# Flamingo gated block on one core: row centring and one rounding cast on GpSimd, and the last quarter of a hand-laid order laid anew

## The chip, the cores and the metric

The kernel runs on one core of one Trainium2 chip. The metric is device time of one execution in microseconds (us), the median of several runs. The engines are called as in the profile: PE (TensorE matmul) with PEld (its weight loads), DVE (VectorE), ACT (ScalarE), POOL (GpSimd) and SP (SyncE, which here only issues DMAs).

## What is computed

The reference, cut to what matters (16 sequences of 224 rows, 512 wide; a context of 750 rows of 384 each, masked at its end; 8 heads of 64; a feed-forward of 2048):

```python
def attention(x, context, mask, W_q, W_k, W_v, W_o, b_o):
    q, k, v = heads(x @ W_q), heads(context @ W_k), heads(context @ W_v)
    sim = where(mask, q @ k.T * 64**-0.5, -max)
    return merge(softmax(sim) @ v) @ W_o + b_o

def bitlinear(x, w, b):                     # ternary weights, rows in 8 bits
    xq = act_quant(rmsnorm(x))              # scale 127 / max|row|, round
    return xq @ weight_quant(w).T + b

x = x + tanh(g_xattn) * attention(layernorm(x), ctx, mask, ...)
n = layernorm(x)
x = x + tanh(g_ffn) * bitlinear(gelu(bitlinear(n, w1, b1)), w2, b2)
```

## The kernel before

The 3584 rows of `x` are 28 tiles of 128 rows, in 14 pairs (0 to 13). Keys that the mask removes are not gathered, so a sequence (a "slot" s, 0 to 15, sorted by length) has at most `CAPS[s]` keys. Attention goes by slot: context transposes (`ctxp`), keys (`kp`), values (`vp`, `vr`), queries (`qp`), scores (`sim`), row maxima with the mask on DVE (`max`), exponentials on ACT (`exp`), reciprocals on DVE (`rec`), the division on POOL (`mul`, L1426), transposes of the probabilities (`ptp`, evicted by `pT`), the weighted sum (`av`, evicted by `xoT`, two halves one after the other).

The rest goes by pair i and tile k (named `step.i.k`):

- `op`: output projection on PE (L1547); `ya`: its gate and residual into `y` on DVE (L1554); `bs`: row mean and variance on DVE (L1591, L1592).
- `fx` (L1595 to L1600): rows less their mean, 128x512, which ACT or DVE writes.
- `ax` (row maximum of |fx|, L1605, and its scale), `xi` (scaled rows to int16, L1614) on DVE; `xq`: these integers cast to bf16 by ACT (L1014) or DVE (L1012); `xqT`: transposed, by a DMA from SP's queue (L1627), and for pair 13 by PE (`xqp`, L1655) and an ACT copy (L1659).
- `c1`: five small POOL instructions for the row scales; `yb`: bias added into `y` on POOL (L1646).
- `hp.i.k.g`: up projection, half g of the 2048 columns, 8 matmuls of 512 columns on PE (L1671); `h`: its eviction with scale and bias on DVE (L1682); `gelu` on ACT (L1726; for pair 13 in halves, L1778); `ah` or `am`: row maximum on DVE (L1731, L1783); `hi`: scaled rows to int16, 128x2048, on DVE (L1737).
- `hq` (L1739 to L1742): those integers cast to bf16, 128x2048, by ACT or DVE as the order says; `hqT`: transposed by a DMA from SP's queue (L1748); for tile 12.0 and pair 13 by halves on PE (`hqp`, L1709) and an ACT copy (L1713). `sq`: row squares on ACT; `c2`: row scales on POOL.
- `fp`: down projection, 16 matmuls (L1908; for 12.0 and pair 13 in two halves `fp.i.k.g`); `yf`: scale and residual on DVE (L1931); `out`: rows to memory, by an indirect DMA from POOL up to pair 11 (L1940) and from SP's queue after (L1938).

Every step is a small function kept by name. The string `ORDER` lists 2263 names; the program is the steps called in that order, and a suffix `:s` or `:v` sends an eviction or cast to ACT or DVE:

```python
names = ORDER.split()
with tc.manual_schedule():
    for name in names:
        key, _, on = name.partition(":")
        steps[key](*on)
```

So each engine's queue is the list with the other engines' steps left out, and an engine never passes over an instruction that waits. What steps of different engines wait for is data and buffers. Two rings of PSUM matter: `ps_sim` has two wide buffers, which `sim`, `av` and `hp` take in turn, so each waits for the eviction of the one before the last; `ps_gen` has four for all else.

Of the kernel before, what the change touches and what calls it, by code (L numbers as in the profile page):

```python
# [12 lines left out]
ALU = mybir.AluOpType  # L13
# [40 lines left out]
wd.1.0 load.b2 pT.1.1.r:s keys.4 ptr.1.2 pT.1.2:s wq.1.7 ptp.1.3 wT.1.2:s ptr.1.3 op.0.0 wi.1.5 wd.1.7 wT.1.6:s wq.1.5
max.2.0.0 wd.1.5 load.b1 gates wT.1.3:s pT.1.3.r:v max.2.0.1 pT.1.2.r:v pT.1.3:s stats.4.1 wT.1.0:s av.1 max.2.0.2
wT.1.1:s wT.1.7:v wT.1.5:s max.2.0.3 ctxp.3.0 ind.5 xoT.1.1:s y.0.0 sim.2.2 xoT.1.0:s ctxp.3.2 exp.2.0.2 sim.2.3 y.0.1
exp.2.0.3 op.0.1 exp.2.0.1 max.2.2.0 exp.2.0.0 max.2.2.3 max.2.3.0 ctxT.3.0:s yo.0.0 max.2.2.2 exp.2.2.3 max.2.2.1
exp.2.2.2 ctxT.3.2:v max.2.3.2 yo.0.1 ya.0.0 exp.2.3.2 sim.2.1 exp.2.2.0 rec.2.0 pi.5 stats.5.0 mul.2.0 kp.3.0
# [3 lines left out]
mul.2.1 ptr.2.2 vr.3 pT.2.2.r:s rec.2.3 mask.3 qT.3.0:s mul.2.3 fx.0.1:s sim.3.0 kT.3.2:s ax.0.0 sim.3.1 v_rest.3:s  # L62
ptr.2.1 ptp.2.1 pT.2.1.r:s ptp.2.2 xi.0.0 c1.0.0 pT.2.1:s ptp.2.3 max.3.0.0 pT.2.2:s ctxp.4.0 xi.0.1 ptr.2.3 exp.3.0.0
qp.3.2 max.3.1.0 xq.0.0:s max.3.0.2 yb.0.1 max.3.1.3 pT.2.3.r:s xqT.0.0 max.3.0.1 pT.2.3:s max.3.0.3 ctx.5.0 exp.3.0.1
max.3.1.1 exp.3.0.2 max.3.1.2 pi.6 av.2 stats.5.1 rstd.4 ctxT.4.0:s exp.3.1.3 ind.7 exp.3.0.3 norm.4.0 y.1.1 xnp.7
xoT.2.0:s hp.0.0.0 xnT.7.4:s xoT.2.1:s exp.3.1.1 hp.0.0.1 qT.3.2:s h.0.0.0 rec.3.0 keys.6 mul.3.0 hp.0.1.0 h.0.0.1
yo.1.1 gelu.0.0 ptp.3.0 h.0.1.0 xnp.8 ptr.3.0 ctxp.4.2 norm.4.1 sim.3.2 pT.3.0:v sim.3.3 x.6.0 max.3.2.0 op.1.0
max.3.3.0 max.3.3.2 xnT.8.5:s y.2.0 exp.3.1.0 max.3.3.3 max.3.2.1 max.3.2.3 yo.1.0 max.3.2.2 exp.3.1.2 max.3.3.1
ah.0.0 xnT.8.4:s hp.0.1.1 exp.3.2.3 exp.3.3.3 exp.3.2.2 qp.4.0 pT.3.0.r:s exp.3.2.0 h.0.1.1 exp.3.2.1 exp.3.3.0 hi.0.0
ctxT.4.2:s exp.3.3.2 exp.3.3.1 op.1.1 rec.3.1 stats.6.0 gelu.0.1 mul.3.1 rec.3.2 ya.1.0 x.6.1 rec.3.3 mul.3.3 kp.4.0  # L70
qT.4.0:s ya.1.1 mul.3.2 ptr.3.1 kT.4.0:v kT.4.0.c:s ptp.3.1 ptp.3.3 pT.3.1.r:s bs.1.1 ptr.3.3 yb.0.0 pT.3.3:s vp.4
# [4 lines left out]
exp.4.0.3 xqT.1.0 exp.4.1.3 exp.4.0.1 xnp.10 yf.0.0 x.7.1 fp.0.1 xnT.10.6:s ind.8 exp.4.0.0 rstd.6 exp.4.1.2  # L76
xnT.10.5:s exp.4.1.0 c1.1.0 exp.4.1.1 rec.4.0 stats.7.0 hp.1.0.0 qT.4.2:v mul.4.0 yf.0.1 hp.1.0.1 h.1.0.0 ctx.6.0
ptp.4.0 h.1.0.1 yo.2.1 hp.1.1.0 pT.4.0:s gelu.1.0 out.0.1 hp.1.1.1 h.1.1.0 yo.2.0 ctxp.5.0 h.1.1.1 sim.4.3 yb.1.0
# [5 lines left out]
ptr.4.3 v_rest.5:v ptp.4.1 fx.2.1:v fp.1.0 mask.5 max.5.0.0 ax.2.0 sq.1.1 hqT.1.1 xi.2.0 qp.5.2 xi.2.1 pT.4.1:s c2.1.1  # L84
max.5.0.3 pT.4.3.r:s max.5.1.0 xq.2.0:s max.5.0.2 yf.1.0 xqT.2.0 max.5.0.1 kp.5.2 rec.4.2 exp.5.0.1 max.5.1.3 mul.4.2
exp.5.0.3 max.5.1.1 max.5.1.2 xnp.11 yb.1.1 kT.5.2.c:s fp.1.1 qT.5.2:s kT.5.2:s ctx.6.1 xnT.11.6:s x.8.0 c1.2.0 xnp.12
yf.1.1 ptr.4.2 xnT.12.7:s hp.2.0.0 exp.5.1.1 xnT.12.6:s exp.5.0.2 yb.2.1 hp.2.0.1 pT.4.2.r:s h.2.0.0 exp.5.0.0
exp.5.1.0 out.1.1 exp.5.1.2 ptp.4.2 h.2.0.1 exp.5.1.3 pi.8 xnp.13 pT.4.2:s ctxp.6.0 sim.5.3 rec.5.0 ctxT.6.0:s mul.5.0
av.4 gelu.2.0 max.5.3.0 max.5.3.3 keys.8 max.5.3.1 yo.3.0 rec.5.1 max.5.3.2 hp.2.1.0 x.9.0 xoT.4.0:v xoT.4.1:v yo.3.1
# [5 lines left out]
max.6.1.0 mul.5.2 stats.9.0 pT.5.3.r:s kT.6.2:s pT.5.3:s max.6.0.1 yb.2.0 hq.2.1:v ptr.5.2 ptp.5.2 ax.3.0 pT.5.2.r:s  # L95
hqT.2.1 vr.6 yo.4.0 exp.6.0.1 pT.5.2:s exp.6.0.2 av.5 ind.9 x.9.1 qT.6.2:s c2.2.0 xi.3.0 fp.2.0 max.6.1.1 c1.3.0
xi.3.1 xq.3.0:v stats.8.0 xqT.3.0 max.6.1.2 c2.2.1 exp.6.1.2 pi.9 fp.2.1 exp.6.0.0 keys.9 max.6.1.3 xoT.5.0:s
v_rest.6:v exp.6.0.3 y.4.1 ind.10 exp.6.1.1 xoT.5.1:s x.8.1 hp.3.0.0 yf.2.0 ctx.8.0 norm.7.0 hp.3.0.1 h.3.0.0 rec.6.0
mul.6.0 xnp.14 h.3.0.1 hp.3.1.0 xnT.14.8:s yf.2.1 gelu.3.0 ptp.6.0 out.2.1 h.3.1.0 ctxp.7.0 sim.6.2 yb.3.0 op.4.0
max.6.2.0 max.6.2.3 max.6.2.1 exp.6.2.0 yo.4.1 ctxT.7.0:v max.6.2.2 ah.3.0 yb.3.1 pT.6.0:s exp.6.2.1 ctxp.7.2 sim.6.3  # L100
norm.7.1 exp.6.2.3 ptr.6.0 exp.6.2.2 op.4.1 out.2.0 exp.6.1.0 hi.3.0 exp.6.1.3 ya.4.0 sq.3.0 rec.6.2 max.6.3.0 mul.6.2
bs.4.0 qp.7.0 ya.4.1 y.5.0 hq.3.0:v fx.4.0:v hqT.3.0 max.6.3.2 max.6.3.3 hp.3.1.1 qT.7.0:s rec.6.1 mul.6.1 pT.6.0.r:s
# [7 lines left out]
v_rest.7:s ptp.7.0 ah.4.0 rstd.8 hq.3.1:s ptr.7.0 op.5.1 norm.8.1 max.7.2.0 hqT.3.1 max.7.3.0 max.7.2.2 c2.3.1  # L110
# [3 lines left out]
hq.4.0:v hqT.4.0 mul.7.3 ptr.7.1 x.10.1 yf.3.1 kp.8.0 pT.7.1.r:v fx.5.1:v ptr.7.2 kT.8.0:s ptp.7.1 ax.5.0 ptr.7.3  # L114
pT.7.2.r:s sim.8.0 pT.7.1:s sim.8.1 pT.7.3.r:s ptp.7.2 sq.4.0 mask.8 c1.5.0 max.8.0.0 ptp.7.3 max.8.0.2 qp.8.2
stats.10.0 pT.7.3:s xi.5.0 norm.8.0 max.8.1.0 pT.7.2:s max.8.0.3 max.8.1.3 yb.4.1 exp.8.0.3 max.8.1.1 kp.8.2
stats.10.1 yb.5.1 max.8.1.2 xnp.17 xi.5.1 fp.4.0 xnT.17.9:s yb.4.0 xnT.17.10:s max.8.0.1 xq.5.0:v exp.8.0.1 ah.4.1
xqT.5.0 exp.8.0.2 out.3.1 qT.8.2:s av.7 hi.4.1 y.6.0 xnp.16 xoT.7.0:s hp.5.0.0 y.6.1 xnT.16.9:v xoT.7.1:s sq.4.1
c2.4.0 hp.5.0.1 h.5.0.0 exp.8.1.0 exp.8.0.0 hp.5.1.0 h.5.0.1 kT.8.2:v gelu.5.0 hp.5.1.1 h.5.1.0 rec.8.0 yf.4.0 mul.8.0
vp.8 hq.4.1:v rstd.9 exp.8.1.1 ah.5.0 hqT.4.1 ptp.8.0 norm.9.1 qp.9.0 v.8:s yo.6.1 h.5.1.1 c2.4.1 pT.8.0:v gelu.5.1  # L120
sim.8.2 sim.8.3 max.8.2.0 yo.6.0 op.6.0 qT.9.0:v max.8.2.2 max.8.2.3 out.4.0 hi.5.0 exp.8.2.3 yb.5.0 max.8.2.1
# [802 lines left out]
def compact_path(ctx, tc, sh, x, context, out, late_rows, stages):  # L924
# [3 lines left out]
    nc = tc.nc  # L928
# [14 lines left out]
    NPAIR = NTOK // 2  # L943
# [628 lines left out]
    def normalise(i, ks=(0, 1)):  # L1572
        f = pairs[i]
# [144 lines left out]
    def gelu(i, k):  # L1718
# [20 lines left out]
        @step("hq", i, k)  # L1739
        def run(on):  # L1740
            hq = f["hq", k]
            cast(on, hq, hq.bitcast(I16))  # L1742
# [473 lines left out]
```

## Time and profile before

| what | value |
|---|---|
| median of 3 runs | 658.07 us (657.64 to 658.19) |
| the profiled execution's own time | 658.56 us |
| its span (first to last instruction) | 656.8 us |
| PE, PEld busy | 633.6 us (96%), 411.8 us (63%) |
| DVE, ACT, POOL busy | 494.2 us (75%), 434.7 us (66%), 380.8 us (58%) |

Busy time of an engine is a share of the whole span. The last 55 us have another make-up than the rest: attention is over, and PE has two pairs of the feed-forward left, whose rows must pass DVE, ACT and POOL before PE can go on.

### The profile page before, as it was taken

What the parts mean: (1) busy time and instruction counts of PE and PEld (TensorE: products, weight loads), DVE (VectorE), ACT (ScalarE), POOL (GpSimd) and SP (SyncE); (2) the same over time, 40 slices, a digit from 0 to 9 for tenths busy, and PEclk for the clock granted to TensorE, in tenths of its full rate; (3) what the DMA queues carried; (4) which work ended last, traced back from release to release, by engine and by line L of the source; (5) the groups of instructions that cost most, each with busy time, mean ns of one, the idle gap of its engine ahead of it and who ended that gap; (6) DMA issues with size and microseconds to landing.
All of it is one profiled execution on the core that took longest, in us unless ns stands there. A gap on an engine that the chain in (4) does not pass through costs nothing.

```text
span 656.8 us, 11053 instructions
## 1 busy us (share of the span) xinstructions
PE 633.6 (96%) x3706; PEld 411.8 (63%) x3706; DVE 494.2 (75%) x1325; ACT 434.7 (66%) x985; POOL 380.8 (58%) x531
## 2 busy tenths in 40 slices
PE   6989899999999999999999999999999999999995
PEld 5767757767566585675756668656666755654442
DVE  6798788776874787777878577886595865858994
ACT  2489786767676673596757467875496554859694
POOL 6444558664866447663757763753776364564741
PEclk9999999999999999999999999999999999999999
DMA  6959682116233053312235521513243041433222
GB/s 204 371 81 304 196 199 69 45 49 110 66 87 86 32 80 91 84 34 61 65 77 80 96 75 34 92 46 58 64 117 73 17 97 50 95 65 81 48 33 86
DMA packets 97346, 60.73 MB, mean 92 GB/s; under 512 B 85461, under 2 KB 85609, under 8 KB 97152
## 3 DMA queue, kind: packets, MB, share of 16 engines
q1 hardware_dynamic: 89232, 35.41, 25.8%
q0 software_dynamic: 8048, 24.53, 12.4%
q8 instruction: 31, 0.51, 0.3%
q14 instruction: 35, 0.29, 0.1%
HBM read 31.87 MB, written 7.34 MB: 60 GB/s over the span
## 4 chain that ended last, share of the span: by engine, by line
PE 84%; DVE 6%; DMA 5%; ACT 2%; issue 1%; POOL 1%; DVEq 0%; POOLq 0%
PE hp L1671 14%; PE fp L1908 14%; PE qp L1345 14%; PE op L1547 13%; PE kp L1180 5%; PE vp L1207 5%; PE sim L1378 5%; PE ptp L1448 3%; PE av L1488 3%; DMA raw<-w 2%; PE xnp L1323 2%; DMA raw<-in_L_ffn_w_dram 2%; PE vr L1224 1%; DMA x<-in_x_dram,token 1%; PE ctxp L1160 1%
## 5 line engine op out<-in xcount | busy, mean ns | idle before, releaser
L1426 POOL TENSOR_TENSOR p<-p,rec 112x752 f32<-112x752 f32 (+13 forms) x64 | 73.2, 1149 | 134.4 <-DVE rec L1421 101.6
L1409 ACT ACTIVATE p<-p,nm 112x188 f32<-112x188 f32 (+13 forms) x256 | 102.0, 401 | 26.8 <-DVE nm L1395 25.8
L1345 PE MATMUL qp<-xnT,wq_sb 128*128 128x224 f32 x512 | 103.2, 355 | 0.0
L1671 PE MATMUL hp<-w1T,xqT 128*128 128x512 fp8e4 x448 | 102.1, 379 | 1.1 <-DVE h L1682 0.7
L1908 PE MATMUL fp<-w2T,hqT 128*128 128x512 fp8e4 x448 | 100.9, 379 | 0.7 <-ACT hqT L1713 0.7
L1547 PE MATMUL op<-wo_sb,xoT 128*128 128x512 f32 x224 | 101.0, 596 | 0.0
L1345 PEld LDWEIGHTS qp<-xnT,wq_sb 128*128 128x128 f32 x512 | 95.4, 190 | 4.9 <-issue 2.9
L1682 DVE SCALAR_TENSOR_TENSOR h<-hp,c,b_bc 128x1024 f32<-128x1024 f32 x52 | 66.6, 1282 | 31.3 <-PE hp L1671 26.5
L1671 PEld LDWEIGHTS <-xqT 128*128 128x128 bf16 x448 | 43.5, 98 | 51.3 <-issue 3.4
L1908 PEld LDWEIGHTS <-hqT 128*128 128x128 bf16 x448 | 43.1, 98 | 49.9 <-issue 1.1
L1547 PEld LDWEIGHTS op<-wo_sb,xoT 128*128 128x128 f32 x224 | 41.0, 190 | 44.7 <-issue 43.5
L1395 DVE CUSTOM_DVE_ANT_0 p<-sim,mask 112x64 f32<-112x64 f32 (+12 forms) x224 | 54.9, 281 | 18.7 <-PE sim L1378 12.0
L1731 DVE TENSOR_REDUCE a<-h 128x1 f32<-128x2048 f32 x26 | 59.2, 2277 | 1.1 <-ACT h L1726 1.1
L1726 ACT ACTIVATE h<-h 128x2048 f32<-128x2048 f32 x26 | 49.7, 1913 | 11.6 <-DVE h L1682 11.4
L1180 PE MATMUL kp<-ctxT,wk_sb 128*128 128x188 f32 (+12 forms) x360 | 52.4, 295 | 0.9 <-ACT pT L1025 0.9
L1180 PEld LDWEIGHTS kp<-ctxT,wk_sb 128*128 128x128 f32 x360 | 49.2, 191 | 5.9 <-issue 3.3
L1025 ACT COPY pT<-ptp 128x448 f32<-128x448 f32 (+6 forms) x54 | 28.1, 528 | 32.1 <-PE ptp L1448 30.1
L1409 ACT ACTIVATION_READ_ACCUMULATOR p<-p,nm 112x1 f32 x256 | 48.7, 190 | 0.0
L1757 ACT ACTIVATE h<-h 128x2048 f32<-128x2048 f32 x25 | 47.8, 1911 | 1.0 <-DVE hq L1737 1.0
L1378 PE MATMUL sim<-kT,qT 64*112 64x188 f32 (+13 forms) x512 | 42.5, 296 | 0.9 <-ACT xoT L1025 0.6
L1646 POOL TENSOR_TENSOR y<-y,b_bc 128x512 f32<-128x512 f32 x28 | 36.1, 1295 | 12.1 <-DVE xoT L1023 9.4
L1207 PE MATMUL vp<-wv_sb,ctxT 128*128 128x512 f32 (+5 forms) x90 | 41.6, 598 | 0.0
(211 smaller groups left out, 1161.4 us busy)
## 6 DMA issues: line engine op xcount, KB each, us to landing
raw<-in_L_ffn_w_dram SPq DMA_DIRECT2D x16, 512.0 KB, 5.5
wq_sb<-in_L_xattn_W_q_dram SPq DMA_DIRECT2D x1, 1024.0 KB
b_bc<-in_L_ffn_b_dram SPq DMA_DIRECT2D x1, 1024.0 KB
wk_sb<-in_L_xattn_W_k_dram SPq DMA_DIRECT2D x1, 768.0 KB
wv_sb<-in_L_xattn_W_v_dram SPq DMA_DIRECT2D x1, 768.0 KB
wo_sb<-in_L_xattn_W_o_dram SPq DMA_DIRECT2D x1, 512.0 KB, 11.6
wo_sb<-in_L_xattn_W_o_dram SPq DMA_DIRECT2D x2, 256.0 KB
out_dram<-y SPq DMA_DIRECT2D x2, 256.0 KB
```

The source lines that it names most:

```text
L1180: nc.tensor.matmul(pk[:, p - p0, :], lhsT=sh.wk[:, c, p * P : (p + 1) * P], rhs=st["ctxT"][:, c, :n], start=(c == 0), stop=(c == NC - 1),)
L1207: nc.tensor.matmul(pv[:w], lhsT=st["ctxT"][:, c, :w], rhs=sh.wv[:, c, :], start=(c == 0), stop=(c == NC - 1))
L1345: nc.tensor.matmul(pq[:, i, :], lhsT=sh.wq[:, d, (p + i) * P : (p + i + 1) * P], rhs=st["xnT"][:, d, :], start=(d == 0), stop=(d == ND - 1),)
L1378: nc.tensor.matmul(sim[:, j, i, :cap], lhsT=st["qT"][j * DH : (j + 1) * DH, p, q * TQ : (q + 1) * TQ], rhs=keys["kT"][j * DH : (j + 1) * D ...
L1395: nc.vector.tensor_tensor_reduce(out=probs[:, h, :cap], in0=box["sim"][:, j, i, :cap], in1=keys["mask"][:, first + j * begin : first + j * ...
L1409: nc.scalar.activation(box["p"][:, h, :cap], box["p"][:, h, :cap], AF.Exp, bias=box["nm", h], scale=-1.0, accum_out=total[:TQ, h : h + 1],)
L1426: nc.gpsimd.tensor_tensor(probs[:, :, first : first + cap], probs[:, :, :cap], box["rec"][:TQ].unsqueeze(2).to_broadcast([TQ, 4, cap]), AL ...
L1547: nc.tensor.matmul(po, lhsT=xoT[:, d, at : at + P], rhs=sh.wo[:, d, :], start=(d == 0), stop=(d == ND - 1))
L1671: nc.tensor.matmul(ph[:, n, :], lhsT=f["xqT"][:, k * ND + d, :], rhs=w1T[:, d, at : at + NB], start=(d == 0), stop=(d == ND - 1),)
L1682: nc.vector.scalar_tensor_tensor(h[:, cols], f["hp", k, g].rearrange("t i n -> t (i n)"), f["c1", k], sh.b1[:, cols], ALU.mult, ALU.add,)
L1731: nc.vector.tensor_reduce(amax[:, part], f["h", k], AX.X, ALU.max, apply_absolute_value=True)
L1908: nc.tensor.matmul(po, lhsT=f["hqT", k][:, n, :], rhs=w2T[:, n, :], start=(n == 0), stop=(n == NF - 1))
```

## The change

For pairs 12 and 13, `fx` is written by POOL (`less_mean("g", k)`), where ACT wrote all four; for pair 12, `hq` is cast by POOL, where ACT cast tile 12.0 and DVE tile 12.1. These six steps no longer take a suffix.

```diff
-            @step("fx", i, k)
-            def run(on, k=k):
+            def less_mean(on, k):
                 less, y, mean = rows("fx")[:, k, :], f["y"][:, k, :], box["mv"][:, k, 0:1]
-                if on == "v":
+                if on == "g":
+                    nc.gpsimd.tensor_scalar(less, y, -1.0, mean, ALU.mult, ALU.add)
+                elif on == "v":
                     nc.vector.tensor_scalar(less, y, -1.0, mean, ALU.mult, ALU.add)
                 else:
                     nc.scalar.activation(less, y, AF.Identity, scale=-1.0, bias=mean)
+
+            if i >= NPAIR - 2:
+                @step("fx", i, k)
+                def run(less_mean=less_mean, k=k):
+                    less_mean("g", k)
+            else:
+                @step("fx", i, k)
+                def run(on, less_mean=less_mean, k=k):
+                    less_mean(on, k)
...
-        @step("hq", i, k)
-        def run(on):
-            hq = f["hq", k]
-            cast(on, hq, hq.bitcast(I16))
+        if i == NPAIR - 2:
+            @step("hq", i, k)
+            def run():
+                hq = f["hq", k]
+                nc.gpsimd.tensor_copy(hq, hq.bitcast(I16))
+        else:
+            @step("hq", i, k)
+            def run(on):
+                hq = f["hq", k]
+                cast(on, hq, hq.bitcast(I16))
```

`ORDER` is written anew from its first line, but most of that moves names of different engines past each other. Split by engine, every queue is as before up to `kp.12.2` on PE; from there 22 further steps move between ACT and DVE (15 evictions, the casts `hq.9.0`, `hq.9.1`, `hq.10.1`, `hq.13.0.0`, `hq.13.0.1`, and `fx.10.1`, `fx.11.1` among them, in both directions), and all queues are in another order. PE's queue from `op.10` on, before and after:

```diff
-op.10.0 ptp.13.1 op.10.1 qp.14.2 sim.14.0 sim.14.1 vp.14 ptp.13.3 xnp.27 fp.9.0 kp.14.2 fp.9.1 hp.10.0.0 hp.10.0.1
-ptp.13.2 hp.10.1.0 hp.10.1.1 ptp.14.0 av.13 ptp.14.1 qp.15.0 sim.14.3 sim.14.2 op.11.0 op.11.1 qp.15.2 fp.10.0
-sim.15.1 sim.15.0 ptp.14.2 ptp.14.3 fp.10.1 av.14 hp.11.0.0 hp.11.0.1 hp.11.1.0 ptp.15.0 ptp.15.1 sim.15.2 sim.15.3
-op.12.1 op.12.0 ptp.15.2 hp.11.1.1 ptp.15.3 av.15 fp.11.0 hp.12.0.0 hp.12.0.1 hp.12.1.0 op.13.0 op.13.1 hp.12.1.1
-hqp.12.0.0 fp.11.1 xqp.13.0 xqp.13.1 hp.13.0.0 hp.13.0.1 hqp.12.0.1 fp.12.0.0 hp.13.1.1 hp.13.1.0 fp.12.0.1
-hqp.13.0.0 hqp.13.0.1 fp.12.1 fp.13.0.0 fp.13.0.1 hqp.13.1.0 hqp.13.1.1 fp.13.1.0 fp.13.1.1
+op.10.0 sim.13.2 sim.13.3 kp.14.0 op.10.1 vp.14 qp.14.2 ptp.13.1 sim.14.0 sim.14.1 fp.9.1 ptp.13.3 fp.9.0 hp.10.0.0
+hp.10.0.1 hp.10.1.0 hp.10.1.1 ptp.13.2 kp.14.2 qp.15.0 av.13 ptp.14.0 sim.14.3 sim.14.2 op.11.1 op.11.0 sim.15.1
+sim.15.0 ptp.14.1 ptp.14.3 ptp.14.2 fp.10.0 qp.15.2 fp.10.1 av.14 hp.11.0.0 hp.11.0.1 hp.11.1.0 sim.15.2 ptp.15.0
+sim.15.3 op.12.0 hp.11.1.1 op.12.1 ptp.15.2 ptp.15.1 ptp.15.3 av.15 fp.11.0 hp.12.0.0 hp.12.0.1 hp.12.1.0 op.13.0
+hp.12.1.1 op.13.1 fp.11.1 hqp.12.0.0 xqp.13.0 hp.13.0.0 hp.13.0.1 xqp.13.1 hp.13.1.0 hp.13.1.1 hqp.12.0.1 fp.12.0.0
+fp.12.0.1 hqp.13.0.0 fp.12.1 hqp.13.0.1 fp.13.0.0 hqp.13.1.0 fp.13.0.1 hqp.13.1.1 fp.13.1.0 fp.13.1.1
```

ACT's queue from the last `pT` on, and POOL's from `mul.15.3` on:

```diff
 ACT
-pT.15.2 pT.15.1 fx.12.0 pT.15.3 fx.12.1 gelu.11.1 xoT.15.1 xq.12.1 xoT.15.0 sq.11.0 sq.11.1 gelu.12.0 hq.11.1
-hq.12.0 fx.13.0 fx.13.1 gelu.12.1 hqT.12.0.0 xq.13.0 xq.13.1 xqT.13.0 xqT.13.1 sq.12.1.1 sq.12.0 gelu.13.0.0
-gelu.13.0.1 sq.12.1.0 hqT.12.0.1 sq.13.0.0 hq.13.0.0 sq.13.0.1 hqT.13.0.0 gelu.13.1.0 gelu.13.1.1 ...
+pT.15.2 pT.15.1 pT.15.3 gelu.11.1 xoT.15.1 xoT.15.0 xq.12.1 sq.11.0 sq.11.1 gelu.12.0 hq.11.1 sq.12.0 gelu.12.1
+xq.13.0 xqT.13.0 sq.12.1.1 xq.13.1 xqT.13.1 hqT.12.0.0 sq.12.1.0 gelu.13.0.0 sq.13.0.0 gelu.13.0.1 sq.13.0.1
+hqT.12.0.1 gelu.13.1.1 gelu.13.1.0 sq.13.1.1 hq.13.0.1 hqT.13.0.0 ...
 POOL
-mul.15.3 y.13.1 c1.12.1 c1.12.0 c2.11.0 yo.13.0 c2.11.1 yb.12.0 yb.12.1 yo.13.1 out.11.0 yb.13.0 c1.13.1 c1.13.0 ...
+mul.15.3 fx.12.0 y.13.0 fx.12.1 c1.12.0 c1.12.1 y.13.1 c2.11.0 yb.12.1 yo.13.0 c2.11.1 yb.12.0 yo.13.1 fx.13.0
+hq.12.0 c1.13.0 fx.13.1 yb.11.1 yb.13.0 c1.13.1 out.11.0 hq.12.1 out.11.1 yb.13.1 c2.12.0 r2.13.0 ...
```

## The prediction

> **What bounds the kernel now.** I read the page's first part for the shares, then the busy times by stage for where PE is not full, then PE's own timeline for what stops it there.
>
> ```profile
> PE 633.6 (96%) x3706; PEld 411.8 (63%) x3706; DVE 494.2 (75%) x1325; ACT 434.7 (66%) x985; POOL 380.8 (58%) x531
> ```
>
> By stage (start and end, length, then busy us of each engine with its instructions, the granted clock, DMA):
>
> ```profile
> 450.00:500.00 50.00, 50.00 (x285) 33.69 (x283) 37.20 (x97) 31.35 (x76) 36.22 (x53) 1.00 0.39 90
> 500.00:550.00 50.00, 50.00 (x290) 30.94 (x289) 31.47 (x94) 28.22 (x76) 22.61 (x38) 1.00 0.24 52
> 550.00:600.00 50.00, 49.93 (x274) 29.01 (x274) 37.57 (x98) 34.69 (x78) 30.65 (x39) 1.00 0.37 78
> 600.00:620.00 20.00, 19.04 (x80) 8.36 (x76) 18.81 (x28) 14.99 (x14) 13.12 (x26) 1.00 0.32 71
> 620.00:640.00 20.00, 19.00 (x116) 9.48 (x116) 19.55 (x30) 19.00 (x26) 10.03 (x28) 1.00 0.19 27
> ```
>
> Up to 600 us PE is full at a full clock: nothing that the other engines do there can be gained, only lost. From 600 on DVE and ACT are nearly full too, and POOL is half idle. PE's timeline there (start, length, count, in brackets the idle time before and who ended it):
>
> ```profile
> 601.39 3.63 PE L1908 MATMUL fp<-w2T,hqT 128*128 128x512 fp8e4 x16
> 605.27 3.63 PE L1671 MATMUL hp<-w1T,xqT 128*128 128x512 fp8e4 x16 [0.25 <-DMA xqT<-xq]
> 609.61 1.89 PE L1671 MATMUL hp<-w1T,xqT 128*128 128x512 fp8e4 x8 [0.71 <-DVE h L1682]
> 611.33 7.03 PE L1547 MATMUL op<-wo_sb,xoT 128*128 128x512 f32 x16
> 618.20 1.89 PE L1671 MATMUL hp<-w1T,xqT 128*128 128x512 fp8e4 x8
> 620.33 0.62 PE L1709 MATMUL hqp<-ident,hq 128*128 128x128 bf16 x8 [0.24 <-ACT hq L1014]
> 620.79 3.62 PE L1908 MATMUL fp<-w2T,hqT 128*128 128x512 fp8e4 x16
> 624.89 0.92 PE L1655 MATMUL xqp<-ident,xq 128*128 128x128 bf16 x8 [0.48 <-ACT xq L1014]
> 625.96 3.63 PE L1671 MATMUL hp<-w1T,xqT 128*128 128x512 fp8e4 x16 [0.16 <-ACT xqT L1659]
> ...
> 637.67 7.07 PE L1908 MATMUL fp<-w2T,hqT 128*128 128x512 fp8e4 x32
> 644.58 1.06 PE L1709 MATMUL hqp<-ident,hq 128*128 128x128 bf16 x16
> 646.29 3.63 PE L1908 MATMUL fp<-w2T,hqT 128*128 128x512 fp8e4 x16 [0.66 <-ACT hqT L1713]
> ```
>
> Fp8 matmuls start 0.216 us apart (32 from 637.67 to 644.58). From `fp.11.0` on PE has 160 of them (34.5 us), two `op` (6.87), 48 `hqp` and 8 `xqp` transposes at 0.056 (3.1): 44.5 us of work. It takes from 601.39 to 649.74 (646.29 plus 16 times 0.216): 48.35 us. So 3.85 us are lost there; that is all that the change can win. After 649.74 come `yf.13.1`, its store and the close of the program, the same in both.
>
> **What leaves and what is added.** ACT loses four `fx` (rows of 0.72, 0.72 and 1.33 for two) and `hq.12.0` (1.90), DVE loses `hq.12.1` (0.68). POOL gains four 128x512 tensor_scalars and two 128x2048 casts. The first have an exact row, the layer norm's:
>
> ```profile
> L1309 POOL TENSOR_SCALAR x<-x,ls_x,rs_x x26: 755/768/1920, 35.1 to 498.7; 128x512 f32<-128x512 f32 x26
> ```
>
> and the row of the bias added (busy us and mean ns after the bar, then idle time before):
>
> ```profile
> L1646 POOL TENSOR_TENSOR y<-y,b_bc 128x512 f32<-128x512 f32 x28 | 36.1, 1295 | 12.1 <-DVE xoT L1023 9.4 <-ACT fx L1600 2.5
> ```
>
> 0.77 us, and 1.92 for the one that lay beside DVE's `hi` (L1737) for 1.27 us. No POOL cast is in the trace. Its price from POOL's 128x1 rows (0.19 us) and a rate per column: iota (0.13 us for 2 columns, 0.30 for 192) gives 2.0 us, tensor_scalar (0.19 to 0.77 over 511 columns) 2.5 us, the two-input tensor_tensor 4.5 us. I take 2.5, the row with one tensor input.
>
> The Trainium skill's GPSIMD Engine Reference (section Elementwise) speaks against moving such work: 4.5 us for a two-input add of 2048 fp32 columns; its section Engine selection calls one-input work roughly line-rate, an estimate of 1.9 us from its 1.03 cycles an element. By the first the sum below would be some 3 us higher, by the second unchanged.
>
> **How much cast PE covers.** `hi.12.0` ends 1.5 us before `op.13.1` (DVE: `ya.13.0`, `bs.13.0`, `hi.12.0` after `op.13.0`; then PE has `hp.12.1.1` and `op.13.1`, 5.2 us). POOL has `fx.13.0` in front; it becomes ready with `hi.12.0` just begun, so it costs 1.9 rather than 0.8, and the cast starts 0.7 us before `op.13.1` ends. `hqp.12.0.0` now stands behind `fp.11.1`: 0.7 + 3.45 = 4.1 us of cover. Behind the cast in POOL's queue wait `c1.13.0` (1.8 us, five small rows) and `fx.13.1` (0.8), which `ax.13.1` needs after `ah.12.1`, 6.2 us after the cast's start: 3.6 us left. `hq.12.1` feeds the transposing DMA (4.3 to 4.9 us from issue to landing), and `fp.12.1` comes 8.9 us after `hi.12.1`: about 3.8 us. So at 2.5 us both casts are free, and above 3.6 us each further 0.1 costs about 0.1. `fx.12.0` and `fx.12.1` wait for `bs` like ACT's did and end before `ax` gets to them; behind them in POOL's queue stand `y.13.0`, `y.13.1` (gathers wanted 10 us later) and `c1`, not late. The `out` stores that POOL's queue moves have no reader, and SP's queue only swaps `hqT.9.0` with `hqT.9.1`.
>
> **The tail in the new order.** Four waits remain.
> (a) `hp.12.1.0` for `h.12.0.0`. From the end of `op.12.1` DVE runs `ya` and `bs` (1.77), `ax.12.0` to `xi.12.1` (3.41, 600.65 to 604.06), `ah.11.1` (2.71), `hi.11.1` (1.20), `h` (1.28), 0.1 for hand-over: 10.5. PE has three `ptp` (1.15), a wait (see below, 0.45), `av` (1.66), `fp.11.0` and two `hp` (6.9), less the 0.16 between last issue and end: 10.0. Lost 0.5.
> (b) The two `xqp` are apart now, each followed by the `hp` that needs it: transposes to their end 0.39, ACT's copy 0.59, two hand-overs 0.12: 1.10, of which 0.22 is work. Twice 0.88 = 1.76; before, both together lost 1.27 (624.24 to 625.96 less 0.45).
> (c) `fp.12.0.1` for ACT's `hqT.12.0.1`. From the start of `xqp.13.1`: 0.46, then ACT in order `xqT` 0.48, `hqT.12.0.0` 0.90, `sq` 1.04, `gelu` 1.12, `sq` 1.15, `gelu` 1.12, `sq` 1.06, `hqT.12.0.1` 0.99, hand-over 0.06: 8.4 us (steps from rows at 623 to 638). PE: 1.10, `hp.13.1.0` and `hp.13.1.1` 3.46, `hqp` 0.45, `fp.12.0.0` 1.73: 6.75. Lost 1.6; nothing but this hand-over was there before.
> (d) `hp.13.1.1` for `h.13.0.1` behind `hi.12.1`: 0.1.
> Sum 3.96 against 3.85: the waits for `xq`, `hq`, the DMA and the last `hqT` go (ACT and DVE are done early behind (c)), and (c) takes their place. +0.1.
>
> **The middle.** The new order has no slack at three places where `ps_sim`'s two buffers turn.
> `sim.14.2` needs `av.13`'s buffer: from `av`'s end ACT's `xoT` 0.53, then DVE's `xoT` 0.62 (row at 583.58, which waited for ACT's), hand-overs 0.18, start to end 0.07: 1.40. Between lie `ptp.14.0` and `sim.14.3`, 0.97 (before `qp.15.0`, 3.0, lay there too). +0.43.
> `sim.15.3` needs `h.11.1.0` (1.28 after `hp.11.1.0`'s end, 1.54 after its last issue); `sim.15.2` and one `ptp` fill 0.99 instead of 1.4. +0.45.
> `av.15` needs `pT.15.1`, second of three copies (0.45 apart) after three `ptp` in a row: 1.6 against 1.15. +0.45.
> All else that moves there (22 evictions and casts between ACT and DVE, `out`, `y`, `yb`, `c2` on POOL) has PE's queue as cover; should one lag, it costs PE its length, 0.5 us.
>
> Sum: +0.43 +0.45 +0.45 +0.1 = +1.4 us. The profiled execution took 658.56 (span 656.8 and 1.76 around it), so 660.0; it lies 0.49 over the median of 658.07, so 659.5. A measurement can tell about 0.2% from no change here, 1.3 us: the limits are 656.75 and 659.39, so the forecast is just on the slow side.
>
> **Rivals.**
> Faster: ACT, 39.7 of 48.6 us busy after 601, was what ended the tail's waits, and 4.7 us of its work go. If its queue then runs ahead of PE by `xqT.13.1`, (a) and (c) vanish: 3.85 - 1.9 = 1.95 less, and with the middle's waits hidden 656.1. For: four of six waits name ACT or a cast. Against: ACT stands waiting for `xqp.13.1`, which is behind `hp.13.0.1` in PE's queue; it decides only if the seven ACT steps of (c) take under 6.8 us. Chance 0.13.
> No change: the hand-overs are shorter than laid out, by 0.1 at each of ten, or the middle's three waits fall away: 658.1 to 659.3. For: PE's timeline shows small overlaps that my rows double. Chance 0.29.
> Worse: the casts run at the two-input rate, 4.5 us, or DVE's `xi`, `hi` block them as 1.92 against 0.77 shows: 1 to 2.5 us over the limit of 3.6, 660.5 to 662.0. For: integers to bf16 is a form without a row. Against: only `xi.13.0` falls into the casts' stretches. Chance 0.15.
> The forecast, 659.4 to 660.4: 0.43. Faster 0.13, same 0.29, slower 0.58. The range, 657.3 to 661.6, leaves out most of the first and the last of the third.
>
> **What would show it.** POOL rows: tensor_scalar 128x512 at 0.77 with one near 1.9, copy 128x2048 near 2.5. PE's timeline: an `fp` of 8 idle 1.6 before it from ACT `hqT`; two `hp` of 16 waiting for `xqT`; a `sim` waiting for DVE `xoT`; no wait of `hqp` for `hq`. A wait of `hqp` or `fp` for POOL, or 3 us off the tail's 48.4, would make it wrong.

## The result and the profile after

The changed kernel took 658.79 us (median of 20 runs, 657.38 to 660.64), the kernel before 656.93 (median of 20, 655.80 to 658.34): ratio 1.003, 95% interval 1.0022 to 1.0037, that is 2.0 us slower (1.4 to 2.4). Single executions of one kernel differ by 2.5 us (before) and 3.3 us (after). So the span of one profile decides nothing here: the profiled execution of after is even the shorter one (span 655.7 against 656.8). What helps is that all queues are the same up to `kp.12.2`. I count from its first matmul to the first matmul of `fp.13.1.0`, and split at `fp.11.0`. The two ends in PE's timeline (start, length, count, in brackets the idle time before), first before, then after:

```profile
477.44 1.47 PE L1180 MATMUL kp<-ctxT,wk_sb 128*128 128x92 f32 x12
```

```profile
475.62 1.47 PE L1180 MATMUL kp<-ctxT,wk_sb 128*128 128x92 f32 x12
...
601.65 3.63 PE L1930 MATMUL fp<-w2T,hqT 128*128 128x512 fp8e4 x16
...
646.56 3.62 PE L1930 MATMUL fp<-w2T,hqT 128*128 128x512 fp8e4 x16
```

Before: 646.29 - 477.44 = 168.85 us, of which 123.95 up to `fp.11.0` at 601.39 (the middle) and 44.90 behind it (the tail). After: 646.56 - 475.62 = 170.94, of which 126.03 and 44.91. The whole loss of 2.09 us between these two profiles lies in the middle; the tail takes as long as it did. The start of `kp.12.2` itself lies anywhere from 475.62 to 478.07 in the fourteen profiles of this study: this is where single executions differ, and no queue differs there.

The shares hardly move; POOL has 5.2 us more (the six moved steps take 7.5 us, other rows of POOL got shorter):

```profile
PE 634.2 (97%) x3706; PEld 412.6 (63%) x3706; DVE 494.8 (75%) x1324; ACT 432.9 (66%) x980; POOL 386.0 (59%) x537
```

By stage (start and end, length, then busy us of PE, PEld, DVE, ACT, POOL, the granted clock, DMA):

```profile
500.00:550.00 50.00, 49.14 (x267) 29.05 (x264) 32.99 (x98) 27.62 (x68) 23.03 (x37) 1.00 0.27 63
550.00:600.00 50.00, 49.16 (x274) 28.98 (x271) 35.58 (x96) 35.25 (x79) 22.59 (x34) 1.00 0.27 63
600.00:620.00 20.00, 19.62 (x83) 8.98 (x84) 18.84 (x28) 14.35 (x13) 16.77 (x29) 1.00 0.35 70
620.00:640.00 20.00, 17.37 (x103) 8.45 (x101) 19.25 (x30) 16.61 (x25) 17.55 (x30) 1.00 0.28 54
```

PE is no longer full from 500 to 600: 0.86 and 0.84 us are missing, where before had 0.00 and 0.07. In the tail ACT has less to do between 620 and 640 (16.61 against 19.00), DVE is as full as it was. PE's waits after:

```profile
501.00 3.61 PE L1930 MATMUL fp<-w2T,hqT 128*128 128x512 fp8e4 x16 [0.86 <-DVE keys L1105]
...
561.02 0.61 PE L1378 MATMUL sim<-kT,qT 64*112 64x64 f32 x8 [0.26 <-DVE xoT L1023]
...
589.15 0.61 PE L1378 MATMUL sim<-kT,qT 64*112 64x64 f32 x8 [0.31 <-DVE h L1695]
...
599.99 1.73 PE L1488 MATMUL av<-pT,v 64*64 64x224 f32 x16 [0.28 <-ACT pT L1025]
...
605.66 5.35 PE L1684 MATMUL hp<-w1T,xqT 128*128 128x512 fp8e4 x24 [0.38 <-DMA xqT<-xq]
...
624.41 3.63 PE L1684 MATMUL hp<-w1T,xqT 128*128 128x512 fp8e4 x16 [0.68 <-ACT xqT L1672]
627.87 0.39 PE L1668 MATMUL xqp<-ident,xq 128*128 128x128 bf16 x4
628.94 3.67 PE L1684 MATMUL hp<-w1T,xqT 128*128 128x512 fp8e4 x16 [0.68 <-ACT xqT L1672]
...
636.05 1.90 PE L1930 MATMUL fp<-w2T,hqT 128*128 128x512 fp8e4 x8 [1.27 <-ACT hqT L1726]
...
638.30 3.63 PE L1930 MATMUL fp<-w2T,hqT 128*128 128x512 fp8e4 x16
```

Seven of these eight are waits that the prediction laid out or their neighbours; the first one, of `fp.8.1` for `keys.14`, is not in it. It is the longest of the middle.

POOL's rows of four of the six moved steps, and the store between them:

```profile
617.15 1.61 POOL L1597 TENSOR_SCALAR fx<-y,mv_y 128x512 f32<-128x512 f32 x1 [0.67 <-DVE mv_y L1592]
618.72 1.88 POOL L1757 CAST hq<-hq 128x2048 bf16<-128x2048 int16 x1
...
622.89 0.69 POOL L1597 TENSOR_SCALAR fx<-y,mv_y 128x512 f32<-128x512 f32 x1
...
628.59 1.86 POOL L1962 DMA_INDIRECT out_dram<-y,token  x1 [0.46 <-DVE h_last L1695]
630.48 1.90 POOL L1757 CAST hq<-hq 128x2048 bf16<-128x2048 int16 x1
```

The casts take 1.88 and 1.90 us, and no PE wait names POOL. But the second starts 1.00 us after its input (`hi.12.1` ends at 629.48), because POOL's queue has the store `out.11.0` ahead of it.

### The profile page after: what moved, and what is told of

It reads as the page before. It is cut to its first block, busy times and chain, and to the rows that moved or that the text cites. A ratio compares the mean times of both kernels' runs of the same rounds, so it can differ in the third digit from the quotient of the medians.

```text
span 655.7 us, 11059 instructions
## 1 busy us (share of the span) xinstructions
PE 634.2 (97%) x3706; PEld 412.6 (63%) x3706; DVE 494.8 (75%) x1324; ACT 432.9 (66%) x980; POOL 386.0 (59%) x537
## 4 chain that ended last, share of the span: by engine, by line
PE 90%; DVE 4%; ACT 2%; DMA 1%; issue 1%; POOL 1%; DVEq 0%; POOLq 0%; ACTq 0%
PE op L1547 15%; PE hp L1684 14%; PE fp L1930 14%; PE qp L1345 14%; PE kp L1180 6%; PE vp L1207 6%; PE sim L1378 5%; PE av L1488 4%; PE ptp L1448 3%; PE xnp L1323 2%; PE vr L1224 2%; PE ctxp L1160 1%; PE av L1502 1%; PE ptr L1462 1%; DMA x<-in_x_dram,token 1%
## 5 line engine op out<-in xcount | busy, mean ns | idle before, releaser
L1953 DVE SCALAR_TENSOR_TENSOR y<-fp,c,y 128x512 f32<-128x512 f32 x28 | 20.8, 745 | 32.1 <-PE fp L1930 27.6
L1378 PE MATMUL sim<-kT,qT 64*112 64x188 f32 (+13 forms) x512 | 43.9, 302 | 1.0 <-DVE xoT L1023 0.4
```

Of the source, the lines that this page charges most:

```text
L1378: nc.tensor.matmul(sim[:, j, i, :cap], lhsT=st["qT"][j * DH : (j + 1) * DH, p, q * TQ : (q + 1) * TQ], rhs=keys["kT"][j * DH : (j + 1) * D ...
```

## The experiments

Times are differences from the kernel before, run beside each, from the ratio and its 95% interval (20 executions of after, 11 or 12 of the runs at +1.0 or less, 4 to 8 of the others); "trace" is the stretch from `kp.12.2` to `fp.13.1.0` in the one profile, less 168.85, with middle and tail apart.

| run | measured | trace | middle, tail |
|---|---|---|---|
| after | +2.0 (1.4 to 2.4) | +2.09 | +2.08, +0.01 |
| e_eng | +1.0 (0.4 to 1.5) | +0.09 | 0.00, +0.09 |
| e_ord | +5.9 (5.1 to 6.8) | +6.08 | +2.33, +3.75 |
| e_mid_b | +0.3 (-0.3 to 0.9) | +0.67 | 0.00, +0.67 |
| e_mid_a | +2.5 (1.6 to 3.5) | +2.17 | +2.09, +0.08 |
| e_yb | +1.0 (0.3 to 1.8) | +0.83 | +1.16, -0.33 |
| e_hqT | +3.9 (2.8 to 5.1) | +4.22 | +2.09, +2.13 |
| e_fxonly | +4.2 (2.8 to 5.6) | +4.69 | +2.06, +2.63 |
| e_hqonly | +4.5 (3.0 to 6.1) | +3.88 | +2.09, +1.79 |
| e_cast3 | +9.0 (7.9 to 10.1) | +9.91 | +2.07, +7.83 |
| e_eng_hq | +0.4 (-0.2 to 1.0) | 0.00 | 0.00, 0.00 |
| e_eng_fx | -0.6 (-1.3 to 0.1) | -0.04 | 0.00, -0.04 |
| e_five | +0.5 (-0.2 to 1.1) | +0.30 | 0.00, +0.30 |

**Engines and order apart.** In `e_eng` the list of before keeps its order and the six steps lose their suffix; in `e_ord` the list of after gets the old suffixes.

```diff
e_eng, in ORDER of before
-fx.12.0:s ... fx.12.1:s ... hq.12.0:s ... fx.13.0:s ... fx.13.1:s ... hq.12.1:v
+fx.12.0   ... fx.12.1   ... hq.12.0   ... fx.13.0   ... fx.13.1   ... hq.12.1
e_ord, in ORDER of after: the same lines the other way
```

> The order of before (every queue as before), but the four fx of pairs 12 and 13 and both hq of pair 12 run on POOL at the places that the old list gives them. Theory 1 (the loss is in the order, the POOL steps cost nothing): no PE wait names POOL, the waits of hqp.12.0.0 and the first xqp shrink a little because ACT and DVE have less before them; 0.3 us less than before, between -1.0 and +0.3. Rival (the POOL steps themselves cost: blocked beside DVE, or late behind c1 and yb): at least +1.3 us, with a PE wait behind hq.12.0 or behind xq.

> The order of after, but the four fx on ACT, hq.12.0 on ACT and hq.12.1 on DVE as before. Theory 1 (the order was laid for POOL's help and is worse without it): fx.12.1 lies behind gelu.11.1 on ACT (3.2 us) and pushes hp.12.1.0 back by about 2, xqp and hp.13 wait longer: 4 to 6 us over before. Rival (the order alone is what costs, the engines are indifferent): +2.0 us, as after. Second rival (POOL is what costs): 0 to +0.5.

`e_ord` comes out as theory 1 had it: without POOL's help the new order is 5.9 us slower than before. `e_eng` fits neither: +1.0 is above theory 1's range (up to +0.3) and below the rival's (from +1.3, which the interval reaches), while its trace shows +0.09 and the waits of before. Against theory 1, one wait names POOL; it has taken the place of ACT's (0.35 for 0.24):

```profile
618.97 0.62 PE L1722 MATMUL hqp<-ident,hq 128*128 128x128 bf16 x8 [0.35 <-POOL hq L1758]
```

So the new order without POOL's help costs 5.9 us, and POOL's help takes some 4 of them back (5.9 less 2.0). In the old order the same help gives nothing back.

**Middle and tail apart.** Both lists hold the same steps ahead of `fp.11.0` but for a few; the two halves are joined crosswise.

```python
e_mid_b = before[:cut] + [step for step in after if step not in before[:cut]]    # cut at fp.11.0
e_mid_a = after[:cut] + [step for step in before if step not in after[:cut]]
```

> All steps that stand ahead of fp.11.0 in the list of before, in that order (fx.12 on ACT with them), then the rest in the order of after (fx.13 and hq.12 on POOL): middle of before, tail of after. Theory 1 (losses add: 1.7 us in the middle, none in the tail): before + 0, between -0.5 and +0.6. Theory 2 (the tail is a chain through DVE and ACT that absorbs what PE lost ahead of it, so the tail of after is really worse once the middle is not late): +0.9 to +1.3, with the waits for hqT.12.0.1 and the two xqT all there and the hp.12 waits of before as well.

> The reverse: the steps ahead of fp.11.0 in the order of after (fx.12 on POOL), then the rest in the order of before with its engines (fx.13 and hq.12 on ACT and DVE). Theory 1 (losses add): before + 1.7 us, between +1.3 and +2.2. Theory 2 (what PE loses in the middle gives DVE and ACT a lead, and the waits for xqT and h at hp.12 shrink by as much): +0.3 to +0.8, with no wait left at hp.12.0.0 and at most 0.4 at hp.12.1.0.

Theory 1 holds in the main: the middle of after costs 2.5 us under the old tail (just over its range of 1.3 to 2.2; 2.17 in the trace), the tail of after 0.3 behind the old middle. Theory 2 is right for a part, within the traces: in `e_mid_b` the tail takes 0.67 longer than before, since PE now comes to it early and finds the waits of both kernels, first those for pair 12, then the new ones:

```profile
604.21 3.63 PE L1684 MATMUL hp<-w1T,xqT 128*128 128x512 fp8e4 x16 [0.42 <-DMA xqT<-xq]
608.38 1.89 PE L1684 MATMUL hp<-w1T,xqT 128*128 128x512 fp8e4 x8 [0.54 <-DVE h L1695]
...
635.30 1.90 PE L1933 MATMUL fp<-w2T,hqT 128*128 128x512 fp8e4 x8 [1.31 <-ACT hqT L1726]
```

**The wait that was not foreseen.** In both kernels `fp.8.1` takes the buffer of `ps_gen` that `pi.14` had, so it waits until `keys.14` on DVE has read it. Before, `fp.8.0` stood between them on PE and covered 3.46 us; these are the two in one row:

```profile
501.02 7.08 PE L1908 MATMUL fp<-w2T,hqT 128*128 128x512 fp8e4 x32
```

In the new order `xnp.26` (0.44 us) stands in its place and `fp.8.0` comes later. And `keys.14` is late. DVE's rows ahead of it, before:

```profile
496.68 0.23 DVE L1125 TENSOR_SCALAR mask<-place_f,slots 112x80 f32<-112x80 bf16 x1
...
499.21 0.54 DVE L1614 TENSOR_SCALAR xq<-fx,k 128x512 int16<-128x512 f32 x1
499.66 0.45 DVE L1105 TENSOR_SCALAR keys<-pi,first 64x1 int32<-64x1 f32 x2
```

and after, followed by POOL's rows of the same stretch:

```profile
495.29 1.81 DVE L1125 TENSOR_SCALAR mask<-place_f,slots 112x80 f32<-112x80 bf16 x1
...
498.90 1.57 DVE L1627 TENSOR_SCALAR xq<-fx,k 128x512 int16<-128x512 f32 x1
500.40 0.46 DVE L1105 TENSOR_SCALAR keys<-pi,first 64x1 int32<-64x1 f32 x2
```

```profile
495.02 0.80 POOL L1426 TENSOR_TENSOR p<-p,rec 112x368 f32<-112x368 f32 x1
495.78 1.26 POOL L1659 TENSOR_TENSOR y<-y,b_bc 128x512 f32<-128x512 f32 x1
...
498.93 1.26 POOL L1659 TENSOR_TENSOR y<-y,b_bc 128x512 f32<-128x512 f32 x1
```

`mask.13` began inside `mul.12.1` and ended 0.06 us after `yb.9.0`; `xi.9.0` ended 0.28 after `yb.9.1`. The experiment moves the two adds behind `c1.9.0`:

```diff
-... mul.12.1 exp.12.3.2 ax.9.0 v.13:s yb.9.0 xi.9.0 ... fp.8.1 yb.9.1 max.13.0.3 ... c1.9.0
+... mul.12.1 exp.12.3.2 ax.9.0 v.13:s xi.9.0 ... fp.8.1 max.13.0.3 ... c1.9.0 yb.9.0 yb.9.1
```

> After, with POOL's yb.9.0 and yb.9.1 moved behind c1.9.0 in its queue, so that they no longer lie beside DVE's mask.13 and xi.9.0. Theory A (those two DVE instructions, 1.81 and 1.57 us in after, stood still while POOL's 1.26 us adds ran; that made keys.14 late and PE lost 0.86 ahead of fp.8.1): mask near 0.2, xi near 0.5, no wait at fp.8.1, 0.9 us less than after, that is before + 0.7 to + 1.5. Rival B (DVE's own order makes keys late): the wait of 0.86 stays, before + 2.0. Rival C (the wait goes but is given back further on): before + 2.0 with longer waits behind it.

Theory A: `xi` takes 0.49, `mask` 0.60 (0.2 was expected; it still lies beside `mul.12.1`), `keys` is done at 500.75 (23.1 us behind the start of `kp.12.2`, against 22.7 in before and 25.2 in after), and the wait is gone:

```profile
497.35 0.60 DVE L1125 TENSOR_SCALAR mask<-place_f,slots 112x80 f32<-112x80 bf16 x1
...
499.88 0.49 DVE L1627 TENSOR_SCALAR xq<-fx,k 128x512 int16<-128x512 f32 x1
```

The middle is 0.92 shorter than in after, and half of the measured loss is gone (+1.0 for +2.0). That the place of two POOL instructions, and not DVE's new order, makes `keys.14` late is shown; nothing was given back later. That PE's old order would have covered the delay follows from the rows (0.93 against the 3.46 of `fp.8.0`); no run tests it.

**The longest wait of the tail.** `fp.12.0.1` waits 1.27 for ACT's `hqT.12.0.1`. The transposes and the copy are moved up:

```diff
 PE
-hqp.12.0.0 xqp.13.0 hp.13.0.0 hp.13.0.1 xqp.13.1 hp.13.1.0 hp.13.1.1 hqp.12.0.1 fp.12.0.0
+hqp.12.0.0 xqp.13.0 hqp.12.0.1 hp.13.0.0 hp.13.0.1 xqp.13.1 hp.13.1.0 hp.13.1.1 fp.12.0.0
 ACT
-hqT.12.0.0 sq.12.1.0 gelu.13.0.0 sq.13.0.0 gelu.13.0.1 sq.13.0.1 hqT.12.0.1
+hqT.12.0.0 hqT.12.0.1 sq.12.1.0 gelu.13.0.0 sq.13.0.0 gelu.13.0.1 sq.13.0.1
```

> After, with hqp.12.0.1 moved up behind xqp.13.0 on PE and its copy hqT.12.0.1 behind hqT.12.0.0 on ACT: the wait (c) of fp.12.0.1 (1.27 us) and part of the first wait for xqT lose their cause. Theory A (the tail's waits are separate costs): 1.3 to 1.9 us less than after. Rival B (behind op.13.1 the tail is one chain through DVE and ACT for pair 13, and PE waits for it wherever its other work stands): those waits go, a new one of about 2 us stands ahead of hqp.13.0.0 for the cast of hi.13.0, and the time is that of after within 0.6.

Rival B for the mechanism: the wait goes and comes back as 2.10 us ahead of `hqp.13.0.0`. The time is worse than either theory gave, 1.9 over after. The rest is the clock:

```profile
640.10 0.62 PE L1722 MATMUL hqp<-ident,hq 128*128 128x128 bf16 x8 [2.10 <-DVE hq L1012]
640.56 5.30 PE L1933 MATMUL fp<-w2T,hqT 128*128 128x512 fp8e4 x16
```

`fp.12.1` takes 5.30 us for sixteen matmuls that take 3.63 elsewhere. By stage (the value after the five engines is the granted clock):

```profile
638.00:640.00 2.00, 0.00 (x1) 0.00 (x0) 1.83 (x7) 2.00 (x3) 1.64 (x5) 1.00 0.52 155
640.00:642.00 2.00, 1.90 (x12) 1.02 (x13) 2.00 (x4) 2.00 (x4) 1.74 (x6) 0.66 0.00 0
642.00:644.00 2.00, 2.00 (x6) 0.74 (x5) 1.93 (x4) 1.80 (x3) 1.10 (x5) 0.50 0.00 0
644.00:646.00 2.00, 2.00 (x15) 1.01 (x14) 1.90 (x4) 0.00 (x0) 0.00 (x0) 0.98 0.01 4
```

After 2.1 us of nothing and 0.46 us of transposes the clock is at a half for about 3.4 us (1.36, 2.00 and 0.08 us of these three windows), which costs 1.7. Without it the trace would be some 0.5 over after, inside rival B's range.

**Which of POOL's two jobs carries the new order.** `e_fxonly` has `hq.12.0:s` and `hq.12.1:v` in the list of after, `e_hqonly` has `:s` at the four `fx`.

> After, but hq.12.0 back on ACT and hq.12.1 back on DVE; the four fx stay on POOL. Theory (ACT's queue is what the new tail leans on): hq.12.0 puts 1.9 us ahead of xq.13.0 and hq.12.1 0.7 on DVE ahead of am.13.0.0; waits at xqp.13.0 and hp.13.1.1 appear; 1.3 us over after (1.0 to 1.8). Rival (the casts on POOL are themselves late): 0 to -0.5.

> After, but the four fx back on ACT; both hq of pair 12 stay on POOL. Theory: fx.12.1 then stands behind gelu.11.1 on ACT (3.2 us with its table load), xi.12.1 and so DVE's whole queue comes 2 us later, and hp.12.1.0 waits 1.5 to 2.1 more: 2.3 us over after (1.8 to 2.8); with the run that has all six back (5.9 over before) this would make the two parts add up. Rival (ACT has room once the casts are gone): +0.5 at most.

Both: the tail grows by 2.63 with the casts back and by 1.79 with the `fx` back (3.75 with both, so the two overlap by 0.7). In `e_fxonly` PE waits for `xq`, as laid out, and then for DVE's cast `hq.13.0.0`; in `e_hqonly` it waits for `h`, as laid out (the first fence is of `e_fxonly`, the second of `e_hqonly`):

```profile
625.14 0.40 PE L1668 MATMUL xqp<-ident,xq 128*128 128x128 bf16 x4 [0.90 <-ACT xq L1014]
...
641.06 0.62 PE L1722 MATMUL hqp<-ident,hq 128*128 128x128 bf16 x8 [1.30 <-DVE hq L1012]
```

```profile
612.90 1.89 PE L1684 MATMUL hp<-w1T,xqT 128*128 128x512 fp8e4 x8 [1.65 <-DVE h L1695]
```

The size for `e_hqonly` came out (2.5 over after, expected 2.3). That for `e_fxonly` was nearly twice what I expected (2.2 for 1.3): the wait for DVE's cast (1.30) had not been counted. `hq.12.1`, ahead of it in DVE's queue, took 1.61 us there beside one of POOL's adds, where it took 0.68 in before.

**How much cast is covered.** The copies are of integers onto themselves and change nothing.

```diff
+                    whole = hq.bitcast(I16)
+                    for _ in range(2):
+                        nc.gpsimd.tensor_copy(whole, whole)
                     nc.gpsimd.tensor_copy(hq, hq.bitcast(I16))
```

> After, with each of the two POOL casts of pair 12 preceded by two POOL copies of the same 128x2048 integers onto themselves: 5.7 us in the place of 1.9 if a copy costs as much as the cast. Theory (the prediction's cover: 3.6 us for hq.12.0, 3.8 for hq.12.1): the casts of after are hidden with 1.7 and 1.9 us to spare, and what lies over it costs its length: 2.1 us ahead of ax.13.1 or hqp.12.0.0 and 1.9 at fp.12.1 behind the transposing DMA, 2 to 4.2 us over after. Rival (the cover is larger, PE's work hides it): under 0.5 over after. Second rival (there is no cover, the cast in after already costs its length): 7 us over after.

The second rival's number came out (7.0 over after), though not for its reason. Two copies take 3.83 us. PE's two main waits:

```profile
625.16 0.62 PE L1722 MATMUL hqp<-ident,hq 128*128 128x128 bf16 x8 [1.54 <-POOL hq L1761]
...
645.38 5.19 PE L1936 MATMUL fp<-w2T,hqT 128*128 128x512 fp8e4 x16 [3.28 <-DMA hqT<-hq]
```

Of the first 3.83 us PE pays 1.54 at `hqp.12.0.0`: 2.3 were covered, as laid out. Behind the cast `fx.13.1` is late, DVE waits 1.93 us for it ahead of `ax.13.1` (the theory had 2.1), and so `xqp.13.1` and `hp.13` wait as well (0.96, 0.80, 0.50). Of the second 3.85 it pays 3.28: next to nothing was covered. And behind the long wait the clock is at a half once more (5.19 us for `fp.12.1`, so 1.6 of the 7.0). The trace of after has the reason: `hqT.12.1` is issued at 632.40, as soon as the cast ends, and lands 5.9 us later, at 638.3; `fp.12.1` starts at 638.30. In after the second cast lies on the edge.

```profile
hqT<-hq SPq DMA_TRANSPOSE x1, 5.9
```

**The old order with fewer steps on POOL.** `e_eng_hq` has only the casts on POOL, `e_eng_fx` only the `fx`, `e_five` all but `hq.12.1`.

> The order of before, only hq.12.0 and hq.12.1 on POOL (the four fx on ACT). The run with all six on POOL came out 0.4 to 1.5 us over before with a trace that shows only 0.1 of it behind kp.12.2. If the casts are the cause (hq.12.1 takes 1.9 on POOL where DVE took 0.68, and its DMA starts later): +0.5 to +1.2 here and 0 with the fx alone. If neither is: both within 0.4 of before.

> The order of before, only the four fx on POOL (hq.12.0 on ACT, hq.12.1 on DVE). If the fx are the cause of the 0.4 to 1.5 us (a fx stretched beside DVE's bs or hi delays ax, xi and xq): +0.5 to +1.2 here and 0 with the casts alone. If neither is: both within 0.4 of before. If POOL helps at all in the old order, as the first sum had it: -0.2.

> The order of before; the four fx and hq.12.0 on POOL, only hq.12.1 stays on DVE (0.68 us). A version to beat both kernels if there is one here: it frees 4.7 us of ACT and leaves the DMA of hqT.12.1 where it was. If ACT's relief is worth something in the old order: 0.3 to 0.8 us less than before. If PE's waits in the tail hang on DVE (h, ax, xi, hi) and not on ACT: within 0.3 of before, as with the fx alone and with the casts alone. If hq.12.0 on POOL is what made the run with all six slower: +0.4 to +1.0.

None is clear of before. The +1.0 of `e_eng` falls apart into +0.4 and -0.6; no profile shows a place for it, and what it is stays open. No version here beats the kernel before by more than its interval.

## Why the prediction came out as it did

**Sign and size.** Forecast +1.4 us; measured +2.0 (1.4 to 2.4). The forecast time of 659.5 stood on a median of three runs (658.07); over twenty the kernel before is 1.1 lower (656.93). A base 1.1 too high and a loss some 0.5 too small cancel in part, so that 658.79 is only 0.7 off; that is luck. By its time 658.79 even lies in what the prediction gave to "no change" (658.1 to 659.3), but against its own base the kernel is slower, clear of noise.

**The middle's three waits** came nearly as worked out, by start-to-start intervals against the shortest of the same steps in any profile:

| place | forecast | measured |
|---|---|---|
| `sim.14.2` for `xoT.13.1` | 0.43 | 0.42 |
| `sim.15.3` for `h.11.1.0` | 0.45 | 0.52 |
| `av.15` for `pT.15.1` | 0.45 | 0.35 |
| `fp.8.1` for `keys.14` | not seen | 0.93 |

Together that is 2.22 for a middle that lost 2.08; before had a little of it too (its `sim.15.2` and `sim.15.3` took 1.21 us where such a pair elsewhere takes 0.93). The 0.45 for `sim.15.3` does not come out of the prediction's own 1.54 and 0.99, which give 0.55. The first three are read from the rows; no run takes one of them away.

**The step that failed** is the sentence "All else that moves there ... has PE's queue as cover". It looked at each moved step's own length. It did not ask what POOL's moved adds would lie beside: `yb.9.0` and `yb.9.1` came to lie on `mask.13` and `xi.9.0`. Nor did it see that PE's queue had lost its cover at that place, `fp.8.0`. It put the middle at 1.33, and it came to 2.08; the sum still fell inside the range, which is wider than that. The prediction had priced the same effect in the tail (1.9 instead of 0.8 for `fx.13.0` beside `hi.12.0`, measured 1.61), with POOL as the one that stands still. In the middle it was DVE that stood still.

The Trainium skill's page SBUF — State Buffer, section SBUF: two separate sides, says that DVE and GpSimd share a pair of ports as an exclusive lock, held for a whole instruction: a DVE instruction in a two-port mode, or with two inputs in SBUF, and a GpSimd one block each other, and whichever starts first goes on. Whether `mask.13` and `xi.9.0` ran in such a mode no run here shows. The rows agree for `xi.9.0` (0.03 us ahead of `yb.9.1` by the profile's starts, ended after it) only if its start is that of a blocked instruction; `mask.13`, blocked behind one POOL instruction, did not get in ahead of the next either.

**The tail** was forecast at +0.1 and measured at +0.01. (a) did not come; in its place `hp.12.0.0` waits 0.38 for the DMA of `xqT`, instead of 0.5 at `hp.12.1.0`. (b): from `xqp` to `hp` 1.07 each (627.87 to 628.94), forecast 1.10. (c): 8.2 us from `xqp.13.1` to `fp.12.0.1` (627.87 to 636.05), forecast 8.4, idle 1.27 for 1.6. (d) did not show. Of the waits of before that were to go, those for `xq`, `hq` and the last `hqT` are gone; the one for the DMA stayed (0.25 before).

**Prices.** Cast 1.88 and 1.90, taken 2.5 between bounds of 2.0 and 4.5; `fx` 0.69, 0.68, 1.61 and 0.69, taken 0.77 and 1.9. The iota row's 2.0 was the nearest of the prices from rows. The prediction's estimate of 1.9 from the Trainium skill's GPSIMD Engine Reference was nearer still. Its section Engine selection says only that one-input work runs roughly at line rate; the 1.03 cycles an element stand in section Elementwise, and at the page's 1.2 GHz they give an estimate of 1.76 us for 2048 columns. The 4.5 us that the page has for two inputs is not this instruction's price. Nor would it have made the sum 3 us higher: by the prediction's own cover it is 0.9 over the 3.6 us of one cast and 0.7 over the 3.8 of the other.

**Cover.** 4.1 us for `hqp.12.0.0` is right: 1.9 of cast and 2.3 left. 3.8 us for `hq.12.1` is wrong: 1.9, all of it used. From `hi.12.1` to `fp.12.1` there were 8.8 us, as laid out (8.9). But 1.0 of them went to `out.11.0`, of which the prediction said only that the stores have no reader: they have none, but this one stands ahead of `hq.12.1` and holds POOL until 630.45. And the DMA took 5.9 us instead of 4.3 to 4.9 (the 25 such DMAs of before take 4.3 to 6.0). It hardly reached the time because the cast took 1.9; at the 2.5 of the prediction PE would have waited some 0.6 more.

**The rivals.** "No change" did not happen: the hand-overs and the three waits were not shorter than laid out by as much as it needed. "Faster" needed ACT to run ahead of PE. ACT did have room (16.61 of 20 us), and `e_hqT` shows why that is worth nothing: take (c) away and DVE's chain for pair 13 is next, 2.10 us. "Worse" by the casts did not happen; `e_cast3` shows that the second cast had no spare time left for it. That the change does what it says is seen in `e_ord`: without POOL its order loses 4 us more.

## What to carry to other kernels

When an order is laid anew, go through the pairs of instructions that newly lie beside each other on GpSimd and VectorE, not only through each one's own wait: two adds of 1.26 us that nobody waited for cost PE 0.93 where it had lost its cover. Ask of a step that moves to another engine what stands ahead of it in that queue, stores without a reader too. And count an engine's relief only after naming the engine that is next: here ACT was relieved and DVE set the tail.

## What the runs showed of the hardware

A PE wait can cost more than its length. In the tail, waits of 1.27, 1.54 and 1.65 us left the granted clock at 1.00. 2.10 us, with 0.46 us of transposes behind it, were followed by about 3.4 us at 0.50, which cost 1.7 more; 3.28 us were followed by the same (`fp.12.1` in 5.19 instead of 3.63). The length alone does not decide it. Near the start of the kernel the same wait, with the same steps behind it, left the clock alone in before and was followed by the half clock in after, where it was the shorter one:

```profile
37.50 0.35 PE L2024 MATMUL wtotp<-wtot,ones 128*128 128x1 f32 x2 [2.73 <-DVE wtot L2019]
38.00:40.00 2.00, 2.00 (x22) 1.70 (x22) 1.86 (x7) 1.45 (x6) 0.77 (x2) 1.00 0.00 0
```

```profile
36.90 0.35 PE L2046 MATMUL wtotp<-wtot,ones 128*128 128x1 f32 x2 [2.60 <-DVE wtot L2041]
38.00:39.00 1.00, 1.00 (x7) 0.67 (x7) 0.97 (x3) 0.45 (x2) 0.16 (x1) 0.50 0.00 0
```

(Each time PE's row and then the window behind it; the first fence is of before, the second of after.) What decides between the two is not shown here.

The Trainium skill's page TensorE: Matmul & The Clock Gate, section Why this matters for your kernels, advises to leave no gap of more than about 3 us between bursts of matmuls; here 2.6 us without a matmul proper were enough in `e_hqT`, and 2.73 us of waiting were not in before. Its section Part 4: PE-mode transpose says that transposes do not count as PE-busy for the clock in the same way, which would fit the 0.46 us; no run here separates them.

VectorE can stand still for GpSimd: a `tensor_scalar` of 80 columns took 1.81 us instead of 0.23 beside two of POOL's `tensor_tensor`, one of 512 columns 1.57 instead of 0.49. And the transposing DMA of one 128x2048 tile landed 4.2 to 5.9 us after its issue in the tails of before and after.
